# Four graph layers on one core: a minimum carried from one half row to the next, epsilon on GpSimd, attention scores finished per batch

## The chip, the core and the metric

The kernel runs on one core of a Trainium2 chip. A core has a matrix engine (TensorE, PE in the profile), a vector engine (VectorE, DVE), a scalar engine (ScalarE, ACT), a general engine (GpSimd, POOL) and a queue that issues transfers (SyncE, SP). Each works through its own instructions in order, and they wait for each other by semaphores. The metric is the device time of one execution in microseconds. Three runs of the kernel before took 4707.65, 4713.2 and 4718.09 us; the median is 4713.2 us.

## The reference, cut to what matters

Eight batches of 2048 nodes with 128 features go through four layers that share one adjacency matrix. Each layer normalises its input, clips it at zero, and adds the layer's result to x:

```python
for layer in (L0, L1, L2, L3):
    h = maximum(layernorm(x), 0)
    x = x + layer(h, adj)

# L0 and L3: graph attention. s1[i] and s2[j] are two scores per node
e = leaky_relu(s1[:, None] + s2[None, :], 0.2)
attention = softmax(where(adj > 0, e, very_negative))     # over j
out = attention @ h
# L0 also weighs its input per node, normalises h = x @ W once more (gamma, beta),
# adds h as a residual and applies elu.  There s1 = h @ a1, s2 = h @ a2 of the normalised h.

# L1: attention with 4 heads of 32 features
scores = q @ k.T / sqrt(32);  scores = where(adj == 0, -inf, scores)
out = softmax(scores) @ v @ W_o + b_o

# L2: mean over the neighbours
out = relu(h @ W_self + b_self + mean_of_neighbours(h) @ W_neigh + b_neigh)
```

A layer norm is `(x - mean) / sqrt(var + 1e-5)`, over the 128 features of a node.

## The kernel before, in words

**Tiles.** 128 nodes lie on the partitions. A batch has T = 16 tiles of 128 nodes, handled in G = 4 groups of four tiles.

**The order of the work.** The order on PE, VectorE, ScalarE and GpSimd is written by hand: the program emits instructions in the order in which they stand on each engine (line 1256). The transfers of SP are placed by the framework. Multi-head attention (layer 1) is the main line: `block_steps` (lines 1081 to 1158) cuts each block of 256 rows and one head into 12 sub-steps, six for each tile of 128 rows, by the table ORDER (lines 1071 to 1078). All else is side work that is woven in: layer 2 and layer 3 of the batch before, the maxima and the loop of layer 0 of the batch after, and the preparation of later batches. `work` (line 1298) spreads side steps by their weights; `locked` (line 1333) fixes three main sub-steps to each step of a graph-attention loop and spreads the functions of further steps over cells 1, 3 and 5. A side step is a weight and a tuple of functions; in `locked` each function of the tuple gets a cell of its own.

**The attention pair.** For one tile of 128 rows and one head, TensorE puts scores into two halves of 1024 columns (`scores`, L941). `masked_scores` (lines 949 to 962) lets VectorE add the mask and take the row's minimum, each half in one instruction (L957) followed by a read of the accumulator into `mh`. Each half starts from the constant HIGHEST. L961 then takes the lesser of the two minima into `mn`, and ScalarE's exponential (L965) reads it. There are 512 such tiles, hence 1024 half passes.

**The norms.** `norm_stages` (line 326) gives stages that run on different groups at the same time, the latest stage first. `stats` has VectorE compute statistics per tile (L336), combine them (L338) and add epsilon for the group (L340, tile `ln_ve`). `root` has GpSimd raise that to the power -0.5 (L346, tile `ln_r`). `apply` (L353, VectorE) or `shift` and `apply_relu` (L361, L368) use the result one step later. There are 160 groups in all.

**The scores of graph attention.** `gat_scores` (line 411) is called once for each group. In layer 3 it copies two columns from the projection (L419) and writes `s2n`, the second score scaled, for that group (L429). In layer 0 the two columns are copied at L613 into `ln_z`; once the second norm's mean and root are there, `score` (line 628) calls `gat_scores`, which corrects both columns by the mean (L422, twice), multiplies by the root (L425), adds a constant (L426) and writes `s2n` (L429). `gat_rows` (line 433) later transposes `s2n` (L400), writes it to memory in four transfers (L403) and reads it back over all partitions in one (L406); the maxima (L445) read that. In batches 1 to 7 the stages `scale` (L621) and `shift` (L624) of the same chain run on GpSimd.

Of the kernel before, what the change touches and what calls it, by code (L numbers as in the profile page):

```python
# [15 lines left out]
ALU = mybir.AluOpType  # L16
AX = mybir.AxisListType

P = 128
EPS = 1e-5  # L20
ALPHA = 0.2
BIG = float(2.0**127)
HIGHEST = 3.0e38


UP = float(2.0**80)
# [5 lines left out]
def gnn_kernel(  # L32
# [79 lines left out]
    def small(s, shape, dt=F32):  # L112
        return new(sl if s.startswith("ln_") else sm, s, s, shape, dt)
# [30 lines left out]
    def bc_last(ap, n):  # L144

        return ap.unsqueeze(2).to_broadcast([ap.shape[0], ap.shape[1], n])

    def bc_mid(ap, n):

        return ap.unsqueeze(1).to_broadcast([ap.shape[0], n, ap.shape[1]])  # L150
# [32 lines left out]
    def next_of(name, ts):  # L183
        turns[name] += 1
        return ts[turns[name] % len(ts)]
# [137 lines left out]
        return out  # L323


    def norm_stages(src, dst, relu=False):


        st = {}

        def stats(g):
            s = small("ln_s", (P, 4, 6))
            mv = small("ln_mv", (P, 4, 2))
            t = src(g)
            for k in range(4):
                nc.vector.bn_stats(s[:, k, :], t[:, k, :])  # L336
            for k in range(4):
                nc.vector.bn_aggr(mv[:, k, :], s[:, k, :])  # L338
            ve = small("ln_ve", (P, 4))
            nc.vector.tensor_scalar(ve, mv[:, :, 1], EPS, None, ALU.add)  # L340
            st[g] = (mv, ve)

        def root(g):
            mv, ve = st[g]
            r = small("ln_r", (P, 4))
            nc.gpsimd.tensor_tensor(r, ve, neg_half[:, 0:4], ALU.pow)  # L346
            st[g] = (mv, r)

        def apply(g):
            mv, r = st.pop(g)  # L350
            t, d = src(g), dst(g)
            for k in range(4):
                nc.vector.tensor_scalar(  # L353
                    d[:, k, :], t[:, k, :], mv[:, k, 0:1], r[:, k : k + 1],
                    ALU.subtract, ALU.mult,
                )

        def shift(g):
            mv, r = st[g]
            m = small("ln_m", (P, 4))  # L360
            nc.vector.scalar_tensor_tensor(m, mv[:, :, 0], -1.0, r, ALU.mult, ALU.mult)  # L361
            st[g] = (m, r)

        def apply_relu(g):
            m, r = st.pop(g)
            t, d = src(g), dst(g)
            for k in range(4):
                nc.scalar.activation(  # L368
                    d[:, k, :], t[:, k, :], AF.Relu, bias=m[:, k : k + 1], scale=r[:, k : k + 1]
                )  # L370

        stats.st = st
        return [stats, root, shift, apply_relu] if relu else [stats, root, apply]
# [34 lines left out]
        )  # L408


    def gat_scores(st, g, src, mean=None, r=None):

        if g == 0:
            st["s"] = small("s", (P, T, 2))
            st["s1"], st["s2"] = st["s"][:, :, 0], st["s"][:, :, 1]
            st["s2n"] = next_of("s2n", s2ns)
        s = st["s"][:, 4 * g : 4 * g + 4, :]
        if mean is None:
            nc.vector.tensor_copy(s, src)  # L419
        else:  # L420
            for c in range(2):
                nc.vector.scalar_tensor_tensor(  # L422
                    src[:, :, c], mean, gab[:, c : c + 1], src[:, :, c], ALU.mult, ALU.subtract
                )
            nc.vector.tensor_tensor(src, src, bc_last(r, 2), ALU.mult)  # L425
            nc.vector.scalar_tensor_tensor(  # L426
                s, src, -1.0, bc_mid(gab[:, 2:4], 4), ALU.mult, ALU.add
            )
        nc.vector.tensor_scalar(  # L429
            st["s2n"][:, 4 * g : 4 * g + 4], s[:, :, 1], -1.0 / UP, None, ALU.mult  # L430
        )

    def gat_rows(st):

        st["s2b"] = new(sp2, "s2b", "s2b", (P, N))
        along_free(st["s2n"], st["s2b"], T)
# [143 lines left out]

    def layer0_ahead(b, eng=nc.gpsimd):

        st, h, hT, zs = {}, {}, {}, {}

        def load(g):
            if g not in h:
                h[g] = new(hp3, "h", "h", (P, 4, P))
                nc.sync.dma_start(out=h[g], in_=x_chunk(b, g))

        st["load"] = load  # L590

        def weigh(g):
            for k in range(4):
                t = 4 * g + k
                eng.tensor_scalar(
                    h[g][:, k, :], h[g][:, k, :], nw1[:, t : t + 1], nb[:, t : t + 1],
                    ALU.mult, ALU.add,
                )

        def turned(g):  # L600
            hT[g] = chunk("h0T")
            turn(h.pop(g), hT[g])

        def project(g):
            if g == 0:
                st["haug"] = new(h0p, "h0", "haug", (P, T, P + 1))
                nc.gpsimd.memset(st["haug"][:, :, P : P + 1], 1.0)
            pt = rows_times(hT.pop(g), w0, "ph")

            def read():  # L610
                nc.scalar.copy(hv(g), pt[:, :, 0:P])
                zs[g] = small("ln_z", (P, 4, 2))
                nc.vector.tensor_copy(zs[g], pt[:, :, P : P + 2])  # L613

            later(read)

        def hv(g):
            return st["haug"][:, 4 * g : 4 * g + 4, 0:P]

        def scale(g):  # L620
            eng.tensor_tensor(hv(g), hv(g), bc_mid(gam, 4), ALU.mult)  # L621

        def shift(g):
            eng.tensor_tensor(hv(g), hv(g), bc_mid(bet, 4), ALU.add)  # L624

        norm2 = norm_stages(hv, hv)

        def score(g):
            mv, r = norm2[0].st[g]
            gat_scores(st, g, zs.pop(g), mv[:, :, 0], r)  # L630

        steps = Steps()
        steps.skewed(
            G,
            [load]
            + norm_stages(lambda g: h[g], lambda g: h[g], relu=True)
            + [weigh, turned, project]
            + norm2[:2]
            + [score]
            + norm2[2:]  # L640
            + [scale, shift],
            1.0,
        )
        return st, steps
# [205 lines left out]
    def layer3(b, gap=1):  # L850

        xb = xs[b]
        st, h, hT = {}, {}, {}

        def hdst(g):
            if g not in h:
                h[g] = new(hp3, "h", "h", (P, 4, P))
            return h[g]

        def turned(g):  # L860
            hT[g] = chunk("h3T")
            turn(h.pop(g), hT[g], AF.Relu)

        def project(g):
            if g == 0:
                st["haug"] = new(bp, "big", "haug", (P, T, P + 1))
                nc.gpsimd.memset(st["haug"][:, :, P : P + 1], 1.0)
            pt = rows_times(hT.pop(g), w3T, "ph3")

            def read():  # L870
                nc.scalar.copy(st["haug"][:, 4 * g : 4 * g + 4, 0:P], pt[:, :, 0:P])
                gat_scores(st, g, pt[:, :, P : P + 2])

            later(read)

        pre = Steps()
        pre.skewed(
            G,
            norm_stages(lambda g: xb[g], hdst)
            + [turned, project],  # L880
            1.0,
        )
        pre.add(0.5, settle)
        pre.add(1.0, lambda: gat_rows(st))

        def finish(i0, n, acc, rec):
            for q in range(n):
                it = i0 + q
                xg = xb[it // 4][:, it % 4, :]
                nc.vector.scalar_tensor_tensor(  # L890
                    xg, acc[:, q, 0:P], rec[:, q : q + 1], xg, ALU.mult, ALU.add
                )
                if it % 4 == 3:
                    g = it // 4
                    nc.sync.dma_start(
                        out=out[b, g * 512 : (g + 1) * 512, :].rearrange("(t p) f -> p t f", p=P),
                        in_=xb[g],
                    )
            return []

        return pre, gat_loop(st, finish, True, gap)
# [47 lines left out]
    def masked_scores(blk, t):  # L949

        b = blk["b"]
        e = new(ep, "e", "e", (P, N))
        pm = masks[b, 2 * blk["ib"] + t]
        mh = small("amh", (P, 2))
        for h in range(2):
            c = slice(h * 1024, (h + 1) * 1024)
            nc.vector.tensor_tensor_reduce(  # L957
                e[:, c], blk["sc"][h], pm[:, c], UP, HIGHEST, ALU.add, ALU.min, mh[:, h : h + 1]
            )
        held[0] -= 2  # L960
        nc.vector.tensor_tensor(blk["mn"][:, t : t + 1], mh[:, 0:1], mh[:, 1:2], ALU.min)  # L961
        blk["e"].append(e)

    def exponentials(blk, t):
# [502 lines left out]
```

## Time and profile before

| | |
|---|---|
| median of three runs | 4713.2 us |
| the profiled execution | 4711.7 us |
| its span, first to last instruction | 4709.8 us |
| mean granted TensorE clock | 0.947 |
| L957, half passes, 1024 | 1212.0 us busy, 1220 ns each |
| L961, lesser of two minima, 512 | 81.9 us busy, 160 ns each |
| L340, epsilon, 160 | 27.6 us busy, 173 ns each |
| L346, power on GpSimd, 160 | 218.9 us busy, 1368 ns each |
| L422, score correction, 64 | 29.1 us busy, 495 ns each |
| L425, L426, 32 each | 16.8 and 5.3 us busy, 525 and 167 ns each |
| L429, `s2n`, 64 | 17.8 us busy, 279 ns each |

Times on the page are microseconds of one execution, unless marked ns. A row of the groups names line, engine, operation, written tile and read tiles with their shapes, the count, busy time and mean duration, and then the engine's idle time ahead of these instructions with what ended it. A row of the timeline gives start, busy time, engine, line and operation. The chain that ended last follows the execution back from its last instruction: at each step to what released it, or to the instruction ahead of it on its engine. "Issue" in the chain is time in which an engine waited for nothing that the profile shows. Records of neighbouring VectorE instructions overlap, so a sum of durations is more than the time that they take; the distance from start to start tells that.

### The profile page before, as it was taken

The numbers are of one execution on the slowest core, as the hardware profiler recorded it, in microseconds if no ns is written. First come the engines' busy times: TensorE is split into PE (matmuls) and PEld (weight loads), VectorE is DVE, ScalarE is ACT, GpSimd is POOL, SyncE is SP. The second block draws the span as 40 slices with busy tenths as digits, with TensorE's granted clock in tenths as the row PEclk, the third lists the DMA queues.
The fourth block names the chain that finished last, engine by engine and source line by source line (L and its number), as shares of the span: only waits on it lengthen the run. The fifth ranks groups of instructions, "written<-read, shape, count | busy, mean of one in ns | idle before, by whom it ended". The sixth has DMA issues, their size and how long they took to land.

```text
span 4709.8 us, 87633 instructions
## 1 busy us (share of the span) xinstructions
PE 4100.3 (87%) x33290; PEld 2831.7 (60%) x33290; DVE 3876.3 (82%) x8345; ACT 3622.3 (77%) x5121; POOL 470.3 (10%) x389
## 2 busy tenths in 40 slices
PE   3669998998899988999899988999889998989966
PEld 2636665675656666576665756566665666656635
DVE  5967767888978988788988889788887899758849
ACT  6639985798849888598876988589884998849926
POOL 1120002003100130001300022000310000000000
PEclk6869999999999999999999999999999999999988
DMA  8521123213241233323233132322324123222122
GB/s 300 153 70 52 41 83 99 80 60 103 80 134 51 70 98 96 113 62 97 69 110 92 61 102 85 123 60 69 100 79 135 49 74 103 79 83 60 51 96 73
DMA packets 312194, 423.34 MB, mean 90 GB/s; under 512 B 65318, under 2 KB 181724, under 8 KB 307676
## 3 DMA queue, kind: packets, MB, share of 16 engines
q1 hardware_dynamic: 311264, 417.51, 29.1%
q8 instruction: 263, 4.31, 0.4%
q14 instruction: 159, 1.30, 0.1%
q10 hardware_dynamic: 508, 0.22, 0.0%
HBM read 365.78 MB, written 55.98 MB: 90 GB/s over the span
## 4 chain that ended last, share of the span: by engine, by line
DVE 32%; PE 32%; ACT 25%; issue 6%; DMA 5%; SPq 1%; POOL 0%; ACTq 0%; DVEq 0%; POOLq 0%
DVE e L957 9%; ACT e L965 7%; PE pagg L796 7%; ACT eT L982 7%; PE pt L977 6%; PE gacc L534 6%; ACT ge L508 5%; DVE dump L445 5%; PE sc L941 5%; DVE ge L514 4%; DVE ge L523 4%; PE acc L992 3%; ACT ge L518 3%; DMA ab<-rowd 2%; DVE ln_s L336 1%
## 5 line engine op out<-in xcount | busy, mean ns | idle before, releaser
L957 DVE CUSTOM_DVE_ANT_0 e<-sc,pm 128x1024 f32<-128x1024 f32 x1024 | 1212.0, 1220 | 195.4 <-PE sc L941 190.6
L982 ACT COPY eT<-pt 128x1024 f32<-128x1024 f32 x1024 | 999.7, 1015 | 482.4 <-PE pt L977 480.3
L534 PE MATMUL gacc<-haug,ge 128*128 128x129 f32 x8192 | 1122.6, 288 | 144.5 <-DVE ge L523 112.3
L977 PE MATMUL pt<-ident,e 128*128 128x128 f32 x8192 | 1057.4, 281 | 203.2 <-DVE amh L957 163.1
L534 PEld LDWEIGHTS gacc<-haug,ge 128*128 128x128 f32 x8192 | 1020.1, 199 | 300.1 <-issue 224.3
L977 PEld LDWEIGHTS pt<-ident,e 128*128 128x128 f32 x8192 | 934.8, 145 | 320.3 <-DVE amh L957 198.6
L965 ACT ACTIVATE e<-e,amn 128x2048 f32<-128x2048 f32 x512 | 1033.1, 2018 | 32.8 <-DVE amn L961 32.8
L508 ACT ACTIVATE ge<-ab,s 128x384 f32<-128x384 f32 (+1 forms) x1536 | 805.4, 579 | 110.1 <-DMA ab<-rowd 85.9
L941 PE MATMUL sc<-ks,qr 32*128 32x512 f32 x4096 | 770.7, 661 | 67.1 <-ACT eT L982 47.0
L518 ACT ACTIVATE ge<-ge 128x768 f32<-128x768 f32 (+1 forms) x768 | 597.6, 779 | 147.9 <-DVE ge L514 147.0
L514 DVE TENSOR_TENSOR ge<-ge,ab 128x768 f32<-128x768 f32 (+1 forms) x768 | 666.9, 868 | 44.4 <-ACT ge L508 40.3
L523 DVE SCALAR_TENSOR_TENSOR ge<-mg,ge 128x768 f32<-128x768 fp8e4 (+1 forms) x768 | 667.2, 869 | 31.2 <-ACT ge L518 30.7
L445 DVE CUSTOM_DVE_ANT_0 dump<-s2b,pmg 128x2048 bf16<-128x2048 f32 x256 | 585.8, 2288 | 41.8 <-DMA s2b<-rowd 19.5
L346 POOL TENSOR_TENSOR ln_r<-ln_ve,neg_half 128x4 f32<-128x4 f32 x160 | 218.9, 1368 | 3847.8 <-DVE ln_ve L340 3598.9
L992 PE MATMUL acc<-eT,vv 128*32 128x256 f32 x8192 | 583.4, 395 | 2.6 <-ACT eT L982 2.6
L992 PEld LDWEIGHTS acc<-eT,vv 128*32 128x32 f32 x8192 | 207.0, 110 | 508.4 <-issue 425.8
L941 PEld LDWEIGHTS sc<-ks,qr 32*128 32x128 f32 x4096 | 238.4, 189 | 240.3 <-ACT eT L982 132.0
L796 PE MATMUL pagg<-mt,hm 128*128 128x512 fp8e4 x1536 | 353.7, 381 | 9.3 <-DVE agT L814 9.3
L796 PEld LDWEIGHTS <-hm 128*128 128x128 bf16 x1536 | 147.5, 98 | 187.2 <-issue 33.5
L379 PE MATMUL ptr<-ident,h 128*128 128x128 f32 x512 | 91.3, 304 | 51.8 <-DVE h L353 15.4
L1045 DVE TENSOR_TENSOR aoT<-po,rT 128x256 f32<-128x256 f32 x64 | 27.2, 424 | 127.2 <-ACT rT L1040 127.1
L1008 ACT COPY oT<-acc 128x512 f32<-128x512 f32 x128 | 74.8, 585 | 55.0 <-PE acc L992 55.0
(128 smaller groups left out, 2596.3 us busy)
## 6 DMA issues: line engine op xcount, KB each, us to landing
pmg<-pm_all SPq DMA_DIRECT2D x256, 256.0 KB
mg<-mg_all SPq DMA_DIRECT2D x128, 384.0 KB
pm<-pm_all SPq DMA_DIRECT2D x128, 256.0 KB
qr<-qd SPq DMA_DIRECT2D x1024, 32.0 KB
mt<-mt_all SPq DMA_DIRECT2D x64, 512.0 KB
ab<-rowd SPq DMA_DIRECT2D x64, 384.0 KB
adj<-in_adj_dram SPq DMA_DIRECT2D x16, 1024.0 KB
s2b<-rowd SPq DMA_DIRECT2D x16, 1024.0 KB
```

The costliest lines, as they stand in the source:

```text
L445: nc.vector.tensor_tensor_reduce(dump, st["s2b"], pm, UP, HIGHEST, ALU.add, ALU.min, st["mn"][:, it : it + 1])
L508: nc.scalar.activation(e[:, c, :], gr[k]["s1"], AF.Prelu, bias=st["s2"][:, j : j + 1], alpha=ALPHA)
L514: nc.vector.tensor_tensor(e, e, bc_mid(gr[k]["m"], 2), ALU.subtract)
L523: nc.vector.scalar_tensor_tensor(e, mt, BIG, e, ALU.mult, ALU.min)
L534: nc.tensor.matmul(gr[k]["acc"][:, q, :], e[:, c, q * P : (q + 1) * P], st["haug"][:, j, :], start=(j == 0 and q == 0), stop=(j == T - 1), ...
L796: nc.tensor.matmul(st["pa"], st["hm"][:, j, s, :], st["mt", g, j // 8][:, j % 8, :], start=(j == 0 and s == 0), stop=(j == T - 1 and s == ...
L941: nc.tensor.matmul(blk["sc"][g // 2][:, (g % 2) * 512 : (g % 2 + 1) * 512], blk["q"][r, t * P : (t + 1) * P], ks_t[b, hh][r, :], start=Tru ...
L957: nc.vector.tensor_tensor_reduce(e[:, c], blk["sc"][h], pm[:, c], UP, HIGHEST, ALU.add, ALU.min, mh[:, h : h + 1])
L965: nc.scalar.activation(blk["e"][t], blk["e"][t], AF.Exp, scale=-1.0, bias=blk["mn"][:, t : t + 1], accum_out=blk["ao"]["sum"][:, t, blk["h ...
L977: nc.tensor.transpose(pt[:, c, t, :], blk["e"][t][:, j * P : (j + 1) * P], ident)
L982: nc.scalar.copy(eT, blk.pop(("pt", w)).rearrange("p c t n -> p c (t n)"))
L992: nc.tensor.matmul(pair["acc"][g * HD : (g + 1) * HD, blk["hh"] % 2, :], vv_t[blk["b"], blk["hh"]][:, j, :], blk["eT"][w][:, g, :], start= ...
```

## The change

- In `masked_scores` the second half's minimum starts from the first half's result instead of HIGHEST, and writes the row's minimum straight into `mn`. The instruction that took the lesser of the two is gone.
- In `norm_stages` the addition of epsilon moves from VectorE (in `stats`) to GpSimd (in `root`), as an instruction of its own ahead of the power. For the second norm of layer 0 (`wide`) the statistics and roots of all four groups lie in one tile each.
- `gat_scores` only copies the two columns of a group into the score tile. A new function `gat_ends` does the rest once for all 16 tiles: in layer 0 at the last group's `score`, in layer 3 ahead of `gat_rows`, as a further function of that step.

```diff
-    def norm_stages(src, dst, relu=False):
+    def norm_stages(src, dst, relu=False, wide=False):
...
-            mv = small("ln_mv", (P, 4, 2))
+            if not wide:
+                mv = small("ln_mv", (P, 4, 2))
+            else:
+                if g == 0:
+                    st["all"] = small("mvs", (P, T, 2)), small("rs", (P, T))
+                mv = st["all"][0][:, 4 * g : 4 * g + 4, :]
...
-            ve = small("ln_ve", (P, 4))
-            nc.vector.tensor_scalar(ve, mv[:, :, 1], EPS, None, ALU.add)
-            st[g] = (mv, ve)
+            st[g] = mv
...
         def root(g):
-            mv, ve = st[g]
-            r = small("ln_r", (P, 4))
-            nc.gpsimd.tensor_tensor(r, ve, neg_half[:, 0:4], ALU.pow)
+            mv = st[g]
+            r = st["all"][1][:, 4 * g : 4 * g + 4] if wide else small("ln_r", (P, 4))
+            nc.gpsimd.tensor_scalar(r, mv[:, :, 1], EPS, None, ALU.add)
+            nc.gpsimd.tensor_tensor(r, r, neg_half[:, 0:4], ALU.pow)
...
-    def gat_scores(st, g, src, mean=None, r=None):
+    def gat_scores(st, g, src):
...
+        nc.vector.tensor_copy(st["s"][:, 4 * g : 4 * g + 4, :], src)
+
+    def gat_ends(st, mean=None, r=None):
+
+        s = st["s"]
+        if mean is not None:
             for c in range(2):
                 nc.vector.scalar_tensor_tensor(
-                    src[:, :, c], mean, gab[:, c : c + 1], src[:, :, c], ALU.mult, ALU.subtract
+                    s[:, :, c], mean, gab[:, c : c + 1], s[:, :, c], ALU.mult, ALU.subtract
                 )
-            nc.vector.tensor_tensor(src, src, bc_last(r, 2), ALU.mult)
-            nc.vector.scalar_tensor_tensor(
-                s, src, -1.0, bc_mid(gab[:, 2:4], 4), ALU.mult, ALU.add
-            )
-        nc.vector.tensor_scalar(
-            st["s2n"][:, 4 * g : 4 * g + 4], s[:, :, 1], -1.0 / UP, None, ALU.mult
-        )
+            nc.vector.tensor_tensor(s, s, bc_last(r, 2), ALU.mult)
+            nc.vector.scalar_tensor_tensor(s, s, -1.0, bc_mid(gab[:, 2:4], T), ALU.mult, ALU.add)
+        st["s1"], st["s2"] = s[:, :, 0], s[:, :, 1]
+        st["s2n"] = next_of("s2n", s2ns)
+        nc.vector.tensor_scalar(st["s2n"][:, 0:T], s[:, :, 1], -1.0 / UP, None, ALU.mult)
...
-                zs[g] = small("ln_z", (P, 4, 2))
-                nc.vector.tensor_copy(zs[g], pt[:, :, P : P + 2])
+                gat_scores(st, g, pt[:, :, P : P + 2])
...
         def score(g):
-            mv, r = norm2[0].st[g]
-            gat_scores(st, g, zs.pop(g), mv[:, :, 0], r)
+            if g == G - 1:
+                mv, r = norm2[0].st["all"]
+                gat_ends(st, mv[:, :, 0], r)
...
-        pre.add(1.0, lambda: gat_rows(st))
+        pre.add(1.0, lambda: gat_ends(st), lambda: gat_rows(st))
...
-        mh = small("amh", (P, 2))
-        for h in range(2):
+        mh = small("amh", (P, 1))
+
+        for h, (least, to) in enumerate(((HIGHEST, mh), (mh, blk["mn"][:, t : t + 1]))):
             c = slice(h * 1024, (h + 1) * 1024)
             nc.vector.tensor_tensor_reduce(
-                e[:, c], blk["sc"][h], pm[:, c], UP, HIGHEST, ALU.add, ALU.min, mh[:, h : h + 1]
+                e[:, c], blk["sc"][h], pm[:, c], UP, least, ALU.add, ALU.min, to
             )
         held[0] -= 2
-        nc.vector.tensor_tensor(blk["mn"][:, t : t + 1], mh[:, 0:1], mh[:, 1:2], ALU.min)
```

More of the change, by code (lines that the diff above doesn't have):

```diff
@@ L408, in along_free @@
         )
-    def gat_scores(st, g, src, mean=None, r=None):
+    def gat_scores(st, g, src):
         if g == 0:
             st["s"] = small("s", (P, T, 2))
[L415 to L420, printed above, removed]
+        nc.vector.tensor_copy(st["s"][:, 4 * g : 4 * g + 4, :], src)
+    def gat_ends(st, mean=None, r=None):
+        s = st["s"]
+        if mean is not None:
             for c in range(2):
                 nc.vector.scalar_tensor_tensor(
-                    src[:, :, c], mean, gab[:, c : c + 1], src[:, :, c], ALU.mult, ALU.subtract
+                    s[:, :, c], mean, gab[:, c : c + 1], s[:, :, c], ALU.mult, ALU.subtract
                 )
-            nc.vector.tensor_tensor(src, src, bc_last(r, 2), ALU.mult)
-            nc.vector.scalar_tensor_tensor(
-                s, src, -1.0, bc_mid(gab[:, 2:4], 4), ALU.mult, ALU.add
-            )
-        nc.vector.tensor_scalar(
-            st["s2n"][:, 4 * g : 4 * g + 4], s[:, :, 1], -1.0 / UP, None, ALU.mult
-        )
+            nc.vector.tensor_tensor(s, s, bc_last(r, 2), ALU.mult)
[3 more added lines that the diff above has]
+        nc.vector.tensor_scalar(st["s2n"][:, 0:T], s[:, :, 1], -1.0 / UP, None, ALU.mult)
     def gat_rows(st):
@@ L581, in layer0_ahead @@
     def layer0_ahead(b, eng=nc.gpsimd):
-        st, h, hT, zs = {}, {}, {}, {}
+        st, h, hT = {}, {}, {}
         def load(g):
@@ L624, in shift @@
             eng.tensor_tensor(hv(g), hv(g), bc_mid(bet, 4), ALU.add)
-        norm2 = norm_stages(hv, hv)
+        norm2 = norm_stages(hv, hv, wide=True)
         def score(g):
-            mv, r = norm2[0].st[g]
-            gat_scores(st, g, zs.pop(g), mv[:, :, 0], r)
+            if g == G - 1:
+                mv, r = norm2[0].st["all"]
+                gat_ends(st, mv[:, :, 0], r)
         steps = Steps()
```

## The prediction, made before the changed kernel ran

> **What bounds the kernel now.** I read the page first: busy time, then the chain of work that ended last.
>
> ```profile
> PE 4100.3 (87%) x33290; PEld 2831.7 (60%) x33290; DVE 3876.3 (82%) x8345; ACT 3622.3 (77%) x5121; POOL 470.3 (10%) x389
> ...
> DVE 32%; PE 32%; ACT 25%; issue 6%; DMA 5%; SPq 1%; POOL 0%; ACTq 0%; DVEq 0%; POOLq 0%
> ```
>
> No engine holds the end alone. A microsecond taken from VectorE counts where VectorE is on the chain, about a third of the span, so each edit has to be placed. The timeline of VectorE in a steady stretch gives the attention pair and the end of a norm's statistics (start, busy time, engine, line):
>
> ```profile
> 2003.28 1.22 DVE L957 CUSTOM_DVE_ANT_0 e<-sc,pm 128x1024 f32<-128x1024 f32 x1
> 2004.42 0.09 DVE L957 DVE_READ_ACCUMULATOR2_ANT amh<- 128x1 f32 x1
> 2004.42 1.22 DVE L957 CUSTOM_DVE_ANT_0 e<-sc,pm 128x1024 f32<-128x1024 f32 x1
> 2005.56 0.09 DVE L957 DVE_READ_ACCUMULATOR2_ANT amh<- 128x1 f32 x1
> 2005.68 0.16 DVE L961 TENSOR_TENSOR amn<-amh 128x1 f32<-128x1 f32 x1
> 2005.76 0.87 DVE L336 BATCH_NORM_STATS2 ln_s<-x 128x6 f32<-128x128 f32 x4
> 2006.54 0.36 DVE L338 BATCH_NORM_AGGREGATE ln_mv<-ln_s 128x2 f32<-128x6 f32 x4
> 2006.94 0.17 DVE L340 TENSOR_SCALAR ln_ve<-ln_mv 128x4 f32<-128x4 f32 x1
> 2007.02 0.95 DVE L523 SCALAR_TENSOR_TENSOR ge<-mg,ge 128x768 f32<-128x768 fp8e4 x1
> ```
>
> Two things to see. An independent instruction starts 0.08 us before the record of its predecessor ends, and the accumulator read costs nothing: the second pass starts with it. A dependent one (L961, L340) starts 0.03 to 0.04 us after the end. A dependence costs about 0.12 us.
>
> Then the scores of layer 0, in one of five like stretches (around 1200, 1755, 2310, 2865, 3420 us), and the same stretch in the busy windows (PE, PEld, DVE, ACT, POOL):
>
> ```profile
> 1188.58 1.38 DVE L422 SCALAR_TENSOR_TENSOR ln_z<-ln_mv,gab,ln_z 128x4 f32<-128x4 f32 x2
> 1190.06 0.17 DVE L425 TENSOR_TENSOR ln_z<-ln_z,ln_r 128x8 f32<-128x8 f32 x1
> 1190.26 0.17 DVE L426 SCALAR_TENSOR_TENSOR s<-ln_z,gab 128x8 f32<-128x8 f32 x1
> 1190.46 0.17 DVE L429 TENSOR_SCALAR s2n<-s 128x4 f32<-128x4 f32 x1
> 1190.54 1.22 DVE L957 CUSTOM_DVE_ANT_0 e<-sc,pm 128x1024 f32<-128x1024 f32 x1
> ```
>
> ```profile
> 1160.00:1240.00 80.00, 63.86 (x545) 49.05 (x544) 76.86 (x174) 63.17 (x92) 29.30 (x20) 0.91 0.24 70
> ```
>
> VectorE is at 96% while TensorE and ScalarE have 16 us to spare. Followed through 1180 to 1216 us, the chain is VectorE's alone. The wait before L425 has a form that matters below:
>
> ```profile
> L425 DVEq EVENT_SEMAPHORE  x32: 21/21/21, 48.5 to 3432.2; - x32
> ```
>
> L422 ends at 1189.96 and L425 starts at 1190.06: 0.10 us, where L426 follows L425 after 0.03.
>
> **What the Trainium skill says.** "Perfetto Trace Analysis", Identifying Dependency Chains: an instruction that waits on several engines may get EventSemaphore instructions ahead of it. The trace agrees (32 at L425, which waits for VectorE and for GpSimd). "VectorE: DVE Perf Modes", The DRAIN you can't avoid: a result read by the next instruction of the same engine needs a semaphore, and in its example the semaphore costs nothing extra. The trace differs for dependent neighbours: 0.12 us each, or 0.19 through an EventSemaphore. "SBUF — State Buffer", Who interferes with whom: VectorE with two SBUF inputs and a GpSimd instruction that reads SBUF exclude each other for the whole instruction. The trace agrees: L422 takes 0.22 us at the median, up to 1.25 us beside GpSimd's L621 or L624 (1.18 us).
>
> **Part 1, the second pass starts from the first's minimum.** Removed: 512 minima (L961). Each costs from the read at 2005.56 to the next start at 2005.76, 0.20 us. Added: the second pass waits for the first read. It waits for TensorE too, so in the built order 483 of 512 get an EventSemaphore ahead, on VectorE's own semaphore; the other 29 wait plainly. By the L425 form it starts 0.10 us after the read's end (2004.51), at 2004.61 instead of 2004.42: +0.19. Behind it in the queue stands all of VectorE's work; ScalarE's exponential (L965) waits for its end. The initial value is now a per-partition operand. Rows with such an operand run longer: 332 ns (L1229) against 292 and 286 (L671, L670), 219 at the median (L422) against 163 (L480), so +0.04 to +0.06; bounds 0 and 0.06, taken 0.05. Net: 483 x (0.19 + 0.05 - 0.20) = +19 us, and 29 x (0.12 + 0.05 - 0.20) = -1 us, on VectorE. On the chain stand 155 second passes; 142 go on through L961 and get +0.04, 13 leave before it and get +0.24: 6 + 3 = +9 us. I add 3 for pairs that lie just off the chain: **+12** (bounds: -2 with the operand free, +33 if a third more pairs come on the chain at 0.24).
>
> **Part 2, epsilon on GpSimd.** L340 goes 160 times. The fence shows its price: aggregates end at 2006.90, the next start could be 2006.82 and is 2007.02, 0.20 us; 32 us on VectorE. In the full chain 89 of 160 appear: 17.8 us. GpSimd gets 160 additions of 128x4, a form the trace does not show: bounds 0.12 us (its memset) and 0.91 (L595, 128x128), taken 0.3, and a 0.08 us step to the power behind it. Its start needs no L340 any more (0.04 + 0.17 earlier), so the root is 0.2 us later. The first reader starts under 1 us after the power in 17 of 160 cases, under 0.2 us in 8, and GpSimd is 10% busy: **+2** (0 to +10). GpSimd's queue behind it (L595, L621, L624, L697) slips as little. Lock stalls from four elements: none seen beside the power (L346); at nothing, up to +4.
>
> **Part 3, scores finished once.** Copies stay (L613 now writes the score tile). The four groups of the batch above occupy 0.94, 1.96, 3.85 and 2.62 us from L422 to the next start; the last stays, with 16 columns (+0.05). Removed: 6.75. Not all is saved: at 1197 us L624 holds L422 for 1.1 us, and behind it comes L523, with two SBUF inputs as well, which then waits instead: 1.1 to 2.3 back, taken 1.75. So 5.0 us in each of seven batches and 3 x 0.94 in the first: 38 us on VectorE, 27 of 32 groups on the chain: 32 us. Layer 3 loses 24 of 32 L429 at 0.28 us (0.20 after the copy, 0.08 to the next): 7 us, a quarter on the chain, 2 us. In layer 3 `gat_rows` now falls one main step later, some 1 to 2 us, with its five SP transfers, past a query load on SP in places. The first reader (L445) comes 50 to 52 us after the transpose in six loops, and only in the last two 8 us after it, so +1. The score tile is claimed earlier, but it is one of three and its former reader is a batch and a half back: nothing.
>
> **The sum.** Gains on the chain: 32 + 18 + 2 = 52. I count 85% of the scores (the 16 us of spare beside them) and 55% of the rest (TensorE at 90% runs close behind): 27 + 11 = 38. So -38 + 12 + 2 + 1 = -23 us against the profiled execution: 4711.7 - 23 = 4688.7 (its span is 4709.8; 1.9 us lie around it). The median of the three runs, 4713.2, is 1.5 above that execution: forecast **4690**.
>
> **Rivals.** About 0.2% (9.4 us) is what a measurement here can tell from no change.
> - *The wait in the middle is paid, the tail was hidden* (slower). If 250 pairs pay 0.24 us without getting 0.20 back, +60 replaces +12: 4738. It decides from 158 pairs on (38 / 0.24). For it: 44 first passes are on the chain whose second is not. Against it: 142 of 155 second passes continue through L961. Chance 0.12.
> - *VectorE is freed, TensorE keeps the time.* Only 30% of the 52 arrives, and +15 stands against it: 4711. For it: TensorE's 87% and equal share of the chain. Against it: the five stretches at 96%. Chance 0.22.
> - *All arrives.* 52 passes through, the operand costs nothing, pairs 0: 4663. Chance 0.18.
> - That an edit does nothing is excluded: the built order has 816 fewer compute instructions on VectorE, 160 more on GpSimd, TensorE's and ScalarE's order unchanged.
>
> **Numbers.** Forecast 0.48. Faster 0.48 + 0.18 = 0.66, same 0.22, slower 0.12. The range takes the first case's bounds and reaches into the second and third: 4660 to 4716, leaving out most of the slower rival.
>
> **What will show it.** Part 1: L961's row gone, some 480 more EventSemaphores, the second pass about 0.1 us after the read's end and 0.05 longer. Part 2: L340's row gone, GpSimd's addition under 0.5 us, no new wait for the root. Part 3: a single chain of score instructions per batch, VectorE's windows around 1200 to 3420 us about 5 us shorter. I am wrong if the second pass starts more than 0.25 us after the read, if waits of L965 for VectorE grow well beyond 32.8 us, or if L523 and L514 take over all the lock stalls.

## The result, and the profile after

The changed kernel takes 4685.7 us (median of 6 runs, 4679.5 to 4688.4) against 4711.7 (6 runs, 4707.5 to 4720.1): ratio 0.9941, 95% interval 0.9929 to 0.9954, or 28 us less (22 to 33). The forecast was 4690. Two of its terms were wrong in opposite directions, which the total does not show. From here on a time in us beside a ratio is its distance from 1 times 4713.

The page of the changed kernel, busy times and then the chain that ended last:

```profile
PE 4081.6 (87%) x33290; PEld 2817.6 (60%) x33290; DVE 3799.3 (81%) x7529; ACT 3619.3 (77%) x5121; POOL 541.3 (12%) x549
...
PE 34%; DVE 31%; ACT 23%; issue 6%; DMA 4%; SPq 1%; DVEq 0%; ACTq 0%; POOL 0%; POOLq 0%
```

VectorE has 77 us less to do, GpSimd 71 more, and the span is 26 us shorter (4683.4 against 4709.8). The shares of the chain hardly moved. The attention pair and the end of a norm's statistics, from the timeline of VectorE (line numbers are those of the changed kernel: L957 has become L960, L336 L341, L523 L525):

```profile
2000.30 1.22 DVE L960 CUSTOM_DVE_ANT_0 e<-sc,pm 128x1024 f32<-128x1024 f32 x1
2001.44 0.09 DVE L960 DVE_READ_ACCUMULATOR2_ANT amh<- 128x1 f32 x1
2001.67 1.28 DVE L960 CUSTOM_DVE_ANT_0 e<-sc,pm,amh 128x1024 f32<-128x1024 f32 x1
2002.88 0.08 DVE L960 DVE_READ_ACCUMULATOR2_ANT amn<- 128x1 f32 x1
2002.88 0.87 DVE L341 BATCH_NORM_STATS2 ln_s<-x 128x6 f32<-128x128 f32 x4
```

The second pass no longer starts with the first's read but 0.23 us after it, and lasts 1.28 us instead of 1.22. Over all 512 pairs the distance is 0.228 us at the median (0.224 to 0.230 from the 10th to the 90th percentile). The lesser of the two minima is gone, which gives 0.20 back. What was to be free at the front is dearer than what was saved at the end: 0.228 + 0.065 - 0.195 = +0.10 us for each pair.

The scores of the same batch as in the prediction's fence, now in one chain, and an instruction with two SBUF inputs 11 us behind them:

```profile
1197.40 0.37 DVE L426 SCALAR_TENSOR_TENSOR s<-mvs,gab,s 128x16 f32<-128x16 f32 x2
1197.87 0.99 DVE L429 TENSOR_TENSOR s<-s,rs 128x32 f32<-128x32 f32 x1
1198.90 1.22 DVE L430 SCALAR_TENSOR_TENSOR s<-s,gab 128x32 f32<-128x32 f32 x1
1200.15 0.17 DVE L433 TENSOR_SCALAR s2n<-s 128x16 f32<-128x16 f32 x1
...
1211.39 1.93 DVE L516 TENSOR_TENSOR ge<-ge,ab 128x768 f32<-128x768 f32 x1
```

Four groups of 0.94, 1.96, 3.85 and 2.62 us, 9.4 together, have become one of 2.8 us (1197.40 to 1200.24). GpSimd in the same stretch:

```profile
1197.62 1.19 POOL L622 TENSOR_TENSOR haug<-haug,gam 128x512 f32<-128x512 f32 x1 [5.07 <-DVE haug L357]
1198.89 1.18 POOL L625 TENSOR_TENSOR haug<-haug,bet 128x512 f32<-128x512 f32 x1
...
1210.73 1.78 POOL L625 TENSOR_TENSOR haug<-haug,bet 128x512 f32<-128x512 f32 x1
```

The stalls beside GpSimd have not vanished: L429 and L430 take about a microsecond and end with L622 and L625 (in batches where nothing holds them both take 0.19 us), and L516 takes 1.93 instead of 0.95 beside the next L625. The groups of GpSimd's new addition and of the power behind it, for the ordinary norms (busy, mean ns, idle ahead):

```profile
L349 POOL TENSOR_SCALAR ln_r<-ln_mv 128x4 f32<-128x4 f32 x128 | 75.1, 586 | 3684.1 <-DVE ln_mv L343 3492.3
L350 POOL TENSOR_TENSOR ln_r<-ln_r,neg_half 128x4 f32<-128x4 f32 x128 | 156.0, 1219 | 10.7
```

The addition has a median of 230 ns, but 52 of these 128 take more than 0.4 us (up to 2219), hence the mean of 586. The long ones are stalls: of all 160, 72 take more than 0.35 us, and 70 of those stand beside a VectorE instruction with two SBUF inputs (L525, L516, L447, L767), against 1 of the 88 short ones. VectorE's waits for the root came to 2.8 us at L357 and 4.1 at L365 (1.2 and 2.5 before).

Where along the execution did the 28 us come? I compared the starts of the 512 attention exponentials in the two traces. The lead is 5.4 us at the first; between the 64th and the 384th it jumps by 3.3, 5.6, 4.5, 6.1, 5.7 and 5.1 us in the six stretches where the scores of layer 0 fall, and elsewhere it moves by 1.2 us at most per 16 pairs, up about as often as down (+1.2 in all). Over the last 80 pairs it falls by 7 us. So the scores pay in their places. The next run, without the carried minimum, has +8.0 elsewhere in the same range, more in the six stretches as well (36 us against 30), and falls by 2 over the last 80: the pair costs everywhere.

### The profile page after: what moved, and what is told of

Its sections match the earlier page's. It is cut to its first block, busy times and chain, and to the rows that moved or that the text cites. A ratio compares the mean times of both kernels' runs of the same rounds, so it can differ in the third digit from the quotient of the medians.

```text
span 4683.4 us, 87349 instructions
## 1 busy us (share of the span) xinstructions
PE 4081.6 (87%) x33290; PEld 2817.6 (60%) x33290; DVE 3799.3 (81%) x7529; ACT 3619.3 (77%) x5121; POOL 541.3 (12%) x549
## 4 chain that ended last, share of the span: by engine, by line
PE 34%; DVE 31%; ACT 23%; issue 6%; DMA 4%; SPq 1%; DVEq 0%; ACTq 0%; POOL 0%; POOLq 0%
DVE e L960 9%; PE pagg L798 7%; PE gacc L536 7%; ACT e L967 7%; ACT eT L984 6%; PE pt L979 6%; DVE dump L447 5%; PE sc L943 5%; ACT ge L510 4%; DVE ge L525 4%; DVE ge L516 4%; PE acc L994 4%; ACT ge L520 2%; DVE ln_s L341 1%; DMA ab<-rowd 1%
## 5 line engine op out<-in xcount | busy, mean ns | idle before, releaser
L979 PE MATMUL pt<-ident,e 128*128 128x128 f32 x8192 | 1046.3, 279 | 185.3 <-DVE amh L960 142.1
L967 ACT ACTIVATE e<-e,amn 128x2048 f32<-128x2048 f32 x512 | 1033.0, 2018 | 31.5 <-DVE amn L960 31.5
L943 PE MATMUL sc<-ks,qr 32*128 32x512 f32 x4096 | 763.8, 662 | 69.6 <-ACT eT L984 46.9
L960 DVE CUSTOM_DVE_ANT_0 e<-sc,pm 128x1024 f32<-128x1024 f32 x512 | 623.6, 1218 | 189.5 <-PE sc L943 185.8
L960 DVE CUSTOM_DVE_ANT_0 e<-sc,pm,amh 128x1024 f32<-128x1024 f32 x512 | 657.4, 1284 | 79.9 <-PE sc L943 8.8
L516 DVE TENSOR_TENSOR ge<-ge,ab 128x768 f32<-128x768 f32 (+1 forms) x768 | 665.4, 866 | 40.1 <-ACT ge L510 36.6
L525 DVE SCALAR_TENSOR_TENSOR ge<-mg,ge 128x768 f32<-128x768 fp8e4 (+1 forms) x768 | 665.9, 867 | 26.1 <-ACT ge L520 23.9
L447 DVE CUSTOM_DVE_ANT_0 dump<-s2b,pmg 128x2048 bf16<-128x2048 f32 x256 | 589.5, 2303 | 43.2 <-DMA s2b<-rowd 20.6
L349 POOL TENSOR_SCALAR ln_r<-ln_mv 128x4 f32<-128x4 f32 x128 | 75.1, 586 | 3684.1 <-DVE ln_mv L343 3492.3
L943 PEld LDWEIGHTS sc<-ks,qr 32*128 32x128 f32 x4096 | 235.7, 188 | 237.1 <-ACT eT L984 126.7
L350 POOL TENSOR_TENSOR ln_r<-ln_r,neg_half 128x4 f32<-128x4 f32 x128 | 156.0, 1219 | 10.7
```

The source lines that it names most:

```text
L447: nc.vector.tensor_tensor_reduce(dump, st["s2b"], pm, UP, HIGHEST, ALU.add, ALU.min, st["mn"][:, it : it + 1])
L516: nc.vector.tensor_tensor(e, e, bc_mid(gr[k]["m"], 2), ALU.subtract)
L525: nc.vector.scalar_tensor_tensor(e, mt, BIG, e, ALU.mult, ALU.min)
L943: nc.tensor.matmul(blk["sc"][g // 2][:, (g % 2) * 512 : (g % 2 + 1) * 512], blk["q"][r, t * P : (t + 1) * P], ks_t[b, hh][r, :], start=Tru ...
L960: nc.vector.tensor_tensor_reduce(e[:, c], blk["sc"][h], pm[:, c], UP, least, ALU.add, ALU.min, to)
L967: nc.scalar.activation(blk["e"][t], blk["e"][t], AF.Exp, scale=-1.0, bias=blk["mn"][:, t : t + 1], accum_out=blk["ao"]["sum"][:, t, blk["h ...
```

## The experiments

Each kernel was timed against the kernel before on the same chip. "Second pass starts" is its distance from the start of the first's accumulator read, median of all pairs.

### Parts 2 and 3 without the carried minimum

```diff
-        for h, (least, to) in enumerate(((HIGHEST, mh), (mh, blk["mn"][:, t : t + 1]))):
+        for h in range(2):
...
-                e[:, c], blk["sc"][h], pm[:, c], UP, least, ALU.add, ALU.min, to
+                e[:, c], blk["sc"][h], pm[:, c], UP, HIGHEST, ALU.add, ALU.min, mh[:, h : h + 1]
...
+        nc.vector.tensor_tensor(blk["mn"][:, t : t + 1], mh[:, 0:1], mh[:, 1:2], ALU.min)
```

> The changed kernel with the old attention pair (two independent minima and L961), so parts 2 and 3 without part 1. Theory A (part 1 is a loss: in the profile after, a pair costs 0.228 us of wait plus 0.065 us of longer second pass against 0.195 us of minimum saved, so +0.10 us, some 50 us on VectorE and 15 to 25 us of it on the path): about 4665 us, some 20 us under the changed kernel and 45 under the kernel before. Rival B (the pair's cost is hidden and the measured 26 us are all that parts 2 and 3 give): 4686 us, the same as the changed kernel. Rival C (part 1 is a gain): 4690 to 4700 us.

Measured: 4661.7 us, ratio 0.9886 (0.9873 to 0.9900): 54 us faster (47 to 60), twice the gain of the whole change. The carried minimum takes about 26 us of it away. Theory A holds.

### The carried minimum alone

The kernel before with only this from the diff:

```diff
-        for h in range(2):
+        for h, (least, to) in enumerate(((HIGHEST, mh), (mh, blk["mn"][:, t : t + 1]))):
...
-        nc.vector.tensor_tensor(blk["mn"][:, t : t + 1], mh[:, 0:1], mh[:, 1:2], ALU.min)
```

> The kernel before with part 1 alone. Theory A: slower, +15 to +25 us, 4727 to 4737 us. Rival B: 4712 us, no change. Rival C: 4700 us or less.

Measured: 4737.8 us, ratio 1.0044 (1.0030 to 1.0058): 21 us slower (14 to 27). Part 1 by itself makes this kernel slower.

### Epsilon alone, and the scores alone

The first is the kernel before with only the move of epsilon to GpSimd:

```diff
-            nc.vector.tensor_scalar(ve, mv[:, :, 1], EPS, None, ALU.add)
...
+            nc.gpsimd.tensor_scalar(r, mv[:, :, 1], EPS, None, ALU.add)
```

The second is the changed kernel with the old pair and with epsilon put back on VectorE, so that only the scores of part 3 are left:

```diff
+            nc.vector.tensor_scalar(r, mv[:, :, 1], EPS, None, ALU.add)
...
-            nc.gpsimd.tensor_scalar(r, mv[:, :, 1], EPS, None, ALU.add)
```

> The kernel before with part 2 alone (epsilon on GpSimd). The prediction gave it -18 us on the chain, some -10 arriving and +2 back: 4704 us. Rival: the steps between the score stretches in the pair of profiles show no gain per norm group there (0.1 to 0.6 us lost per 16 pairs), so that VectorE's freed 0.2 us per group is waited away: 4711 us.

> The kernel before with part 3 alone (epsilon stays on VectorE, written into the root's tile). The prediction gave 32 us on the chain, 27 arriving: 4685 us. The pair of profiles shows 3.3 to 6.1 us per batch in the score stretches, 30.2 us over six of them with the second norm's epsilon in it, so 4680 to 4688. If e1 is near 4665 and this is near 4685, epsilon gives the other 20; if this is near 4670, epsilon gives nearly nothing.

Measured: epsilon 4691.2 us, ratio 0.9955 (0.9943 to 0.9968), 21 us (15 to 27). Scores 4681.5 us, ratio 0.9929 (0.9916 to 0.9941), 33 us (28 to 40). Together 54, as in the run that has both: the two add up. Epsilon gave more than twice what I had put in, and neither time expected for it (4704, or 4711 by the rival) came.

### The operand alone, and the wait alone

Both are the kernel before, L961 included, with another second pass: in the first it starts from a column of constants, in the second it starts from HIGHEST but writes over the first pass's column, and so has to wait for it.

```diff
+    high = const.tile([P, 1], F32, name="high")
+    nc.gpsimd.memset(high, HIGHEST)
...
-                e[:, c], blk["sc"][h], pm[:, c], UP, HIGHEST, ALU.add, ALU.min, mh[:, h : h + 1]
+                e[:, c], blk["sc"][h], pm[:, c], UP, high if h else HIGHEST,
+                ALU.add, ALU.min, mh[:, h : h + 1]
```

```diff
-        mh = small("amh", (P, 2))
+        mh = small("amh", (P, 1))
...
-                e[:, c], blk["sc"][h], pm[:, c], UP, HIGHEST, ALU.add, ALU.min, mh[:, h : h + 1]
+                e[:, c], blk["sc"][h], pm[:, c], UP, HIGHEST, ALU.add, ALU.min, mh
...
-        nc.vector.tensor_tensor(blk["mn"][:, t : t + 1], mh[:, 0:1], mh[:, 1:2], ALU.min)
+        nc.vector.tensor_tensor(blk["mn"][:, t : t + 1], mh, mh, ALU.min)
```

> The kernel before, with the second pass starting from a constant of 3.0e38 held per partition instead of in the instruction; L961 stays, no wait is added. Theory A (a pair's cost is 0.065 us of operand in the second pass and 0.19 to 0.23 us of wait): the second pass about 1284 instead of 1220 ns, starting with the first's read as before; 33 us more on VectorE, +10 to +18 us in time, 4726 to 4734. Rival (the longer second pass in the profile after is the wait's doing, not the operand's): second pass 1220 ns, 4715 us.

> The kernel before, with the second pass overwriting the first's minimum in the same column, so that it has to wait for the first's read, as in the changed kernel, but starts from the constant in the instruction; L961 stays. It leaves the first half out of the row's minimum. Theory A: the second pass starts 0.19 us after the read (0.23 in the changed kernel, if part of that is the operand's fetch), 1220 ns long; 97 us more on VectorE, +40 us in time, about 4755. Rival (the wait is mostly hidden behind TensorE, and the operand is what costs): under +10 us.

Measured: operand 4723.9 us, ratio 1.0021 (1.0012 to 1.0029), 10 us slower (6 to 14). Wait 4757.9 us, ratio 1.0095 (1.0081 to 1.0108), 45 us slower (38 to 51). The pair in the timeline of the first, and then of the second:

```profile
2007.28 0.08 DVE L959 DVE_READ_ACCUMULATOR2_ANT amh<- 128x1 f32 x1
2007.28 1.27 DVE L959 CUSTOM_DVE_ANT_0 e<-sc,pm,high 128x1024 f32<-128x1024 f32 x1
2008.48 0.08 DVE L959 DVE_READ_ACCUMULATOR2_ANT amh<- 128x1 f32 x1
```

```profile
2005.01 0.09 DVE L957 DVE_READ_ACCUMULATOR2_ANT amh<- 128x1 f32 x1
2005.24 1.23 DVE L957 CUSTOM_DVE_ANT_0 e<-sc,pm 128x1024 f32<-128x1024 f32 x1
2006.39 0.08 DVE L957 DVE_READ_ACCUMULATOR2_ANT amh<- 128x1 f32 x1
```

With the operand only, the second pass starts with the read and is 0.06 us longer (1278 against 1218 ns at the median). With the wait only, it starts 0.226 us late and has its old length. So in the pair the two costs are separate and add up (the change as made has 0.228 and 1284), and the operand's fetch is no part of the wait.

### The same change with the halves taken in the other order

Nearly every second pass waits for two engines: VectorE for the first minimum, TensorE for its half of the scores. If the half that TensorE writes last is taken first, the later pass needs TensorE no more.

```diff
-        for h, (least, to) in enumerate(((HIGHEST, mh), (mh, blk["mn"][:, t : t + 1]))):
+        for h, least, to in ((1, HIGHEST, mh), (0, mh, blk["mn"][:, t : t + 1])):
```

> The changed kernel whole, but in each pair the second half of the columns is taken first and the first half second. TensorE writes the first half before the second, so what the later pass waits for on TensorE is already covered by the earlier one: in the built order all 512 later passes wait plainly for VectorE, with no EventSemaphore ahead. Theory A (a good part of the 0.228 us is the EventSemaphore): the later pass starts 0.12 to 0.16 us after the read, as other dependent neighbours do, 0.07 to 0.1 us less for 512 pairs is 36 to 50 us of VectorE; at the 45% that arrived before that is 15 to 22 us, and about 5 of it go back because the first pass must wait for the second half's matmuls: 4665 to 4680. Theory B (the wait is the accumulator read's own way back, whatever carries it): it starts 0.22 to 0.23 us after the read as before, and the time is 4685 to 4700.

Measured: 4674.5 us, ratio 0.9909 (0.9895 to 0.9923): 43 us faster than the kernel before (36 to 49), 15 better than the change as made. The pair in its timeline, and its line of EventSemaphores; in the change as made there are 570 at this line:

```profile
2000.96 0.08 DVE L960 DVE_READ_ACCUMULATOR2_ANT amh<- 128x1 f32 x1
2001.08 1.28 DVE L960 CUSTOM_DVE_ANT_0 e<-sc,pm,amh 128x1024 f32<-128x1024 f32 x1
```

```profile
L960 DVEq EVENT_SEMAPHORE  x91: 21/21/2262, 332.2 to 4398.6; - x91
```

The second pass now starts 0.118 us after the read (115 to 120 ns), where it was 0.228. Half of the wait was the dependence, and half, 0.11 us, the second semaphore. But the first pass now needs both halves of the scores: VectorE waits for L943 257.0 us instead of 194.5, where some 5 us had been expected to go back. Theory A holds, in the start and in the time, but most of what was freed (512 x 0.11 = 56 us, 64 by the table below) went into waits of that kind.

### Another instruction between the passes, with and without the carry

The first pass moves one sub-step earlier, and the masking of graph attention (L525) moves from cell 1 to cell 3 of a loop step, so that other VectorE work lies between the two passes in 381 of 512 pairs. The second kernel has the same moves and the old pair with L961.

```diff
-        ["V1"],
-        ["ttr"],
+        ["V1", "ttr0"],
+        ["ttr1"],
...
-            "product": 5, "masked": 1, "exps": 3, "lowered": 1, "leaky": 3,
+            "product": 5, "masked": 3, "exps": 3, "lowered": 1, "leaky": 3,
```

> The changed kernel with the first pass emitted one sub-step earlier and the masking of graph attention (L525) moved between the passes, so that in 381 of 512 pairs at least one other VectorE instruction stands between the first pass and the second. Theory A (the wait is the loss, the removed minimum a true gain): the wait disappears in those pairs, each then costs 0.065 - 0.195 = -0.13 us against the old pair; 36 us less on VectorE than without part 1, some 15 us in time: about 4647, under both kernels. Rival (the order around the pair matters more: the earlier first pass waits for TensorE, the later masking delays its product): over 4670, and its companion without the carried minimum is as slow.

> The companion of e7: the same moved order, but the old pair (two independent minima and L961) with parts 2 and 3. It tells the move from the carry. Theory A: 4662 us, as without the move, and some 15 us over e7. Rival (the order matters more): as far from 4662 as e7 is.

Measured: with the carry 4641.2 us, ratio 0.9844 (0.9830 to 0.9857), 74 us faster (67 to 80); without it 4644.1 us, ratio 0.9855 (0.9842 to 0.9868), 68 us (62 to 74). A pair in the timeline of the first:

```profile
2002.73 0.08 DVE L960 DVE_READ_ACCUMULATOR2_ANT amh<- 128x1 f32 x1
2002.73 0.95 DVE L525 SCALAR_TENSOR_TENSOR ge<-mg,ge 128x768 f32<-128x768 fp8e4 x1
2003.60 1.28 DVE L960 CUSTOM_DVE_ANT_0 e<-sc,pm,amh 128x1024 f32<-128x1024 f32 x1
```

The second pass starts 0.08 us before its neighbour's record ends, like any independent instruction, and so it does in 378 of the 381 pairs: behind other work the wait costs nothing. In the 131 pairs that are still adjacent it starts 0.228 us after the read as before. The gain that Theory A then expected of the carry (some 15 us) does not show, though: the two kernels differ by 5 us, with intervals that overlap. The first time fits Theory A (4647), the second (4662 expected) fits the rival: the moved order matters more than the carry. The next section shows where the carry's gain went. These are the fastest kernels of the study; their gain over parts 2 and 3 alone (14 to 20 us) belongs to the moved order, that is to the earlier first pass, the later masking, or both, which no run separates. VectorE then waits less for ScalarE before `aoT` (52 us against 131) and more for the scores; beyond that I did not follow it.

### Epsilon left out, and epsilon added twice

The first is the kernel before without L340 and with nothing on GpSimd in its place. The second has a second addition behind L340:

```diff
             nc.vector.tensor_scalar(ve, mv[:, :, 1], EPS, None, ALU.add)
+            nc.vector.tensor_scalar(ve, ve, 0.0, None, ALU.add)
```

> The kernel before with epsilon left out altogether: VectorE's addition is gone and none comes on GpSimd; the power reads the variance itself. Theory A (what part 2 brought, 25 us, is VectorE's time alone, and GpSimd's addition costs almost nothing): the same as part 2 alone, 4684 to 4694. Theory B (GpSimd's 0.54 us per addition is felt, but was paid out of a larger gain): 4665 to 4680.

> The kernel before with a second addition (of zero) behind each of the 160 additions of epsilon on VectorE, in place and dependent: about 0.20 us each, 32 us on VectorE, and the power on GpSimd starts 0.2 us later. Theory A (near the norms about four fifths of VectorE's time reaches the end, 25 of 32 us as when the addition was taken away): 20 to 28 us slower, 4733 to 4741. Theory B (the prediction's share, 55% of 17.8 us, is right and taking it away brought more for another reason): 8 to 13 us slower, 4721 to 4726.

Measured: without epsilon 4694.2 us, ratio 0.9958 (0.9945 to 0.9971), 20 us faster (14 to 26); with two additions 4739.8 us, ratio 1.0056 (1.0043 to 1.0069), 26 us slower (20 to 33). The first agrees with epsilon moved to GpSimd (21, 15 to 27): within these intervals GpSimd's addition costs nothing that shows. The second fits Theory A: of 32 us more on VectorE, some four fifths reach the end.

## Why the total was right, and its terms were not

**Where freed or added time goes.** I added up VectorE's gaps of over 0.3 us in the timeline of each profiled execution, before its first and after its last instruction included; the rest of the span is work, short waits included.

| kernel | span | VectorE's gaps | rest |
|---|---|---|---|
| before | 4709.8 | 765.5 | 3944.3 |
| after | 4683.4 | 777.8 | 3905.6 |
| parts 2 and 3 | 4661.5 | 791.2 | 3870.3 |
| carry alone | 4738.2 | 756.7 | 3981.4 |
| wait alone | 4759.2 | 719.0 | 4040.2 |
| other half first | 4675.3 | 833.3 | 3842.0 |
| filled, no carry | 4639.4 | 790.8 | 3848.5 |
| filled, carry | 4640.5 | 829.8 | 3810.7 |

Parts 2 and 3 free 74 us of VectorE (predicted: 32 + 38 + 7 = 77); 26 turn into longer gaps, and 48 reach the end of this execution. The wait alone adds 96; 47 of it are taken out of gaps. In the filled kernels the carry frees 38 us, and the gaps grow by 39: VectorE is freed and something else keeps the time. The chain points to TensorE, though no run tests it: it has 41% there and VectorE 26%, from the page of the filled kernel with the carry:

```profile
PE 41%; DVE 26%; ACT 21%; issue 7%; DMA 4%; SPq 1%; ACTq 0%; DVEq 0%; POOL 0%; POOLq 0%
```

**Part 1: the mechanism right, its price too low.** Predicted +0.04 us a pair and +12 in all; measured +0.10 and +21 to +26. The failed term is the wait, "By the L425 form it starts 0.10 us after the read's end": the second pass starts 0.145 us after it. That L425 reads what an ordinary instruction wrote, and the second pass what an accumulator read wrote, is not the difference: in both the EventSemaphore starts 39 ns after the end of what is waited for and takes 21. From its end L425 starts after 45 ns, the second pass after 85. The trace of before has the same step, where VectorE stood idle until an EventSemaphore ended: CUSTOM_DVE_ANT_0 starts 84 to 85 ns later in 10 first passes of L957, which wait for TensorE and ScalarE, and in 12 instructions of L445, which wait for a transfer; TENSOR_TENSOR and TENSOR_SCALAR start after 44 to 47 ns at the soonest (L425, L827, L1176). So the missing 0.04 us goes with the kind of instruction, and could have been read before. Why it does, and why nothing of it shows without an EventSemaphore (0.118 us after the read's start, as at L961), stays open. The operand, 0.05 taken, is 0.06 to 0.065 (the upper bound given was 0.06). The way from the pair to the end was right: with the measured prices the same sum, 142 x 0.10 + 13 x 0.29 + 3, is 21 (the 3 is still only an estimate). The number of EventSemaphores was right as well, 772 to 1246, that is 474 more (some 480 foreseen). The sign "wrong if over 0.25 us after the read" was set too wide: at 0.228 the pair was already more than twice as dear as thought.

The Trainium skill, "VectorE: DVE Perf Modes", The DRAIN you can't avoid, has an example of eight copies in which a semaphore after each one costs nothing extra. Between the dependent neighbours here a wait does cost: 0.118 us plain and 0.226 to 0.228 through an EventSemaphore, from the read's start to the next start, against 0 for an independent pass.

**Parts 2 and 3: counted right, then discounted a second time.** The chain count gave 32 + 18 + 2 = 52 us; measured are 54 (47 to 60). All of it arrived. The failed step is "I count 85% of the scores (the 16 us of spare beside them) and 55% of the rest (TensorE at 90% runs close behind)". The chain count had already left out 25 of VectorE's 77 us as covered, and 26 us went into longer gaps. To discount 52 again counted the cover twice. Epsilon suffered most: 10 of 17.8 counted, 21 measured (15 to 27). In the other direction more arrives: a second addition costs 26 of 32 us. That added time off the chain counts once it has filled its gap would explain it, but the trace speaks against it: VectorE's gaps in that run are some 3 us longer than before, not shorter. Why more arrives than the chain counts stays open.

GpSimd's part: the addition was put at 0.3 us, its median is 0.23 and its mean 0.59. The sign "under 0.5 us" fails for the mean. "Lock stalls from four elements" were put at nothing, and 72 of 160 additions have them; in before's trace the power has them too (61 of 160 take over one and a half times its median of 1032 ns). It cost nothing that shows, with GpSimd 12% busy. Of the +2 for late roots nothing shows in time (20 without the addition, 21 with it), though VectorE's waits for the root grew by 3.2 us. The lock stalls of the scores were foreseen in place and kind; 1.75 us of them were to come back at L523, and in the batch shown L516 took one of about a microsecond, and the scores' own L429 and L430 two more. The 3.3 to 6.1 us a batch of the whole change (2.3 to 7.2 with the scores alone) stand around the 5.0 worked out. Layer 3's later rows (+1) are below what these runs resolve.

**The rivals.** "All arrives" was right on parts 2 and 3, and wrong on the pair, which it put at 0. "TensorE keeps the time" is wrong for the change as made, and fits the carry once the passes are filled. "The wait in the middle is paid, the tail was hidden" puts the pair at +60, far over the 21 to 26 measured, and by a mechanism that is not needed: the tail was mostly recovered, and the wait with the operand (0.29) was dearer than the tail (0.20). ScalarE's exponential waits for VectorE 31.5 us (32.8 before), as the prediction wanted. Errors of 19 us (gains too small) and of 9 to 14 us the other way (pair too cheap) nearly cancelled: that the total came within 5 us is luck.

**Open.** The pair's median price of 0.10 us gives 50 us over 512 pairs, the table 35 to 37; some of L961's instructions carried stalls of their own (mean 171 ns in the run without the carry, 160 before), and waits under 0.3 us count as rest in the table; how much each explains I did not settle. From the last exponential to the end the kernel before takes 230.2 us, the changed one 233.5 and that with parts 2 and 3 228.8; I count this to no part of the change.

## What to carry to other kernels

Saving an instruction at the end of a pair is no gain if it makes two back-to-back instructions depend on each other: compare the wait that appears with the distance to the next start that goes, and look whether the new dependent already waits for another engine. Here the second semaphore cost as much again as the dependence; another instruction in between took the whole wait away, an order that needs one wait only took half. What such a pair frees is still not gained where another engine is close behind. In this kernel the time counted on the chain needed no second discount. Parts that are right only in sum are best run one by one.

## What the runs showed of the hardware that I had not expected

- A dependent neighbour on VectorE starts 0.118 us after the start of an accumulator read, and 0.226 to 0.228 when it also waits for TensorE through an EventSemaphore; the EventSemaphore's own record is 21 ns, and from its end CUSTOM_DVE_ANT_0 starts after 84 to 85 ns, L425's TENSOR_TENSOR after 45.
- A per-partition initial value makes a pass over 128x1024 0.06 to 0.065 us longer (1278 and 1284 against 1218 ns), whether it was written just before or is a constant.
- GpSimd's addition of 128x4 takes 0.23 us at the median and up to 2.2 us beside VectorE instructions with two SBUF inputs, so four elements are enough for such a stall; 160 of them cost the end nothing that shows.
